# Four layers on four images: the 4x4 convolution for images 3 and 4, exchanged attention operands in fourteen query blocks, and hand-set paces

## The chip, the cores and the metric

The kernel runs on one core of one Trainium2 chip. The metric is device time in microseconds for one execution; the time of the kernel before is the median of three runs. A core has a matrix engine (TensorE, PE in the profile), a vector engine (VectorE, DVE), an activation engine (ScalarE, ACT), a general engine (GpSimd, POOL) and a synchronising engine (SyncE, SP) that here issues DMA transfers. Each engine runs its own instructions in order and waits for others on semaphores. Operands lie in SBUF, products of PE in the eight banks of PSUM, 512 fp32 values per partition each. All data are fp32.

## The reference

Four images of 256 channels and 64x64 pixels pass through four layers, each `x = x + layer(groupnorm32(x))`:

```python
# layer 0: 3x3 convolution, group norm, relu, then attention over all 4096 pixels
xs = relu(group_norm(conv3x3(x, smooth_w) + smooth_b, 8 groups))
g, theta, phi = (conv1x1(xs, w, b) for each)            # 128 channels each
y = softmax(theta^T phi) @ g                             # 4096 x 4096, per image
return 0.1 * group_norm(conv1x1(y, w_w), 32 groups) + xs
# layer 1: linear attention, 4 heads of 32, rms norms before and after
# layer 2: a 3x3 depthwise kernel and a 256x256 pointwise matrix, both generated from the image
# layer 3: softmax-weighted mixture of four 256x256 matrices
```

The softmax needs, for each query pixel, a sum over 4096 keys. Layer 0's attention and convolution are most of the matrix work.

## The kernel before

Channels lie on partitions, in two halves of 128 (`h`). The image being worked on is in `big` and `xp`; intermediate images go through DRAM (`xs_d`, `wy_d`).

**Order of the work.** No scheduler decides the order: the kernel is a Python program that issues instructions in the order in which they go to the engines. Long pieces of work are generators. `attend(b)` is the attention of image `b`: eight query blocks of 512 pixels (`q`), each in 16 steps (`m`) of 256 keys, so 128 steps. A step issues the two logits products of the *next* step (`pf`, L1021), their exponentials on ACT (`pr`, L1022), two products with `g` that accumulate into one PSUM bank (`py`, L1129), and one DVE addition of the probabilities into `tot` (helper line L132). Between two steps of `attend(b)` a `Chain` issues a piece of other work: what is left of image `b-1` (`tail`: `nonlocal_out`, `linear_attention`, generated layer, experts) and then the convolution of image `b+1`. The other work's generators `yield n`, which adds `n * rate` to a credit; each whole credit is one attention step. `yield None` waits for exactly one step, and `later(n, f)` runs `f` after `n` steps. After an image's attention, `project()` makes `theta`, `phi` (`ps_tp`, L957) and `g` (`ps_g`, L962) of the next image. The last image's tail runs with no attention beside it.

**Convolution.** All images use a Winograd form. Image 1 has `convolve_first`. Image 2 (`b == 1`) has `convolve_second`, with tiles of 4x4 outputs in planar layout: 18 products, each a pair of transformed filters times 8 matmuls of 256 columns (`planar_joiner`, L601). Images 3 and 4 have `convolve`, with tiles of 4x2 outputs: 24 products of 4 matmuls of 512 columns (L529). DVE makes the transformed input `v` and joins the products. Transformed filters `u` are read from DRAM a product ahead, on SP's queue in `convolve_second`, on ACT's (L495) in `convolve`. The closing relu (`normed_relu`) is one ACT instruction per 1024 columns (L703), or four strided ones for image 2 (L698).

**End of a query block.** For `q < 7`, `ended_by_dram` writes the sums over 128 partitions to DRAM (`sum_d`), reads them turned, reduces and inverts them, sends them through DRAM again (`rec_d`) so that every partition holds them, multiplies (`yq`) and does the output product `ps_wy` (L1073); some 14 steps lie between its start and end. For `q == 7`, `ended` sums over partitions by a product with ones (`pss`, L1089), and takes a reciprocal of 128x512 on DVE (L1099).

**Statistics** for the group norms are mostly `bn_stats` on DVE. A `guard` array collects the sizes of sums and reciprocals; if they left a range, a general version of the kernel would run after, which in these runs does not happen.

Of the kernel before, what the change touches and what calls it, by code (L numbers as in the profile page):

```python
# [13 lines left out]
P = 128  # L14
# [24 lines left out]
RW = MX * (IX + 1)  # L39

# [6 lines left out]
class Chain:  # L47
# [3 lines left out]
    def __init__(self, layers, rate=1.0, held=()):  # L51
        self.layers, self.rate, self.due = layers(self), rate, []
        self.held, self.unsettled = held, []
# [28 lines left out]
    def steps(self):  # L82
        credit = 0.0
        for part in (self.layers, self.pending()):
            for n in part:
                if n is None:
                    credit += self.rate - 1
                    yield
                    self.tick()
                    continue  # L90
                credit += n * self.rate
                while credit >= 1:
                    credit -= 1
                    yield
                    self.tick()
# [3 lines left out]
def conv_preact_fast(ctx: ExitStack, tc: tile.TileContext, guard, x, wc, wtpg, ww, wqkv, wout, w1cat, wd2,  # L99
# [44 lines left out]
    tpg = cp.tile([P, 3, N], F32, name="tpg")  # L144
    ra = cp.tile([P, NH, IY, RW], F32, name="ra")
    rt = cp.tile([P, NH, IY, RW], F32, name="rt")
    theta, phi, g = tpg[:, 0, :], tpg[:, 1, :], tpg[:, 2, :]
# [106 lines left out]
    tpgf = tpg.rearrange("p k n -> p (k n)")  # L254
# [80 lines left out]
    def stats_tile():  # L335
        return sp.tile([P, NH, 8, 6], F32, name="st")
# [7 lines left out]
    def warm(n):  # L344

        if n:
            ps = bank("ps_warm")
            for i in range(2 * n):
                nc.tensor.matmul(ps[:, 0:P], ones, ident, start=(i == 0), stop=(i == 2 * n - 1))

# [141 lines left out]
    def load_filter(a, k, last):  # L492

        u = filter_tile("u")
        (nc.scalar if last == 3 else nc.sync).dma_start(out=u, in_=rows_d[a, :, :, 0 if k == 0 else 2] if k in (0, last) else filters[a, :, k - 1])  # L495
        return u
# [88 lines left out]
    def planar_joiner(st):  # L585
# [3 lines left out]
        def stats(k):  # L589
            for oh in range(NH):  # L590
                for s in range(2):
                    nc.vector.bn_stats(st[:, oh, 2 * k + s, :], outs[:, oh, k, bass.ts(s, 2), :])

        def products(pair, v, u):
# [9 lines left out]
            if pair != (0, 5):  # L604
                parts[pair] = k4("sums").rearrange("p (k n) -> p k n", k=2)
                nc.scalar.mul(parts[pair][:, 0], banks[0], -1 / 6 if pair == (1, 2) else 1 / 24)
            return banks

        def joined(a, pair, ps, end):
# [11 lines left out]
            elif not end:  # L621
                s = parts[pair]
# [3 lines left out]
            else:  # L626
                near, far = parts[1, 2], parts[3, 4]
# [10 lines left out]
        return products, joined, rows_joined, operations, stats  # L638

    def input_stats():  # L640

        st = stats_tile()
        for h in range(NH):
            for c in range(8):
                nc.vector.bn_stats(st[:, h, c, :], xin[:, h, bass.ts(c, RB), :].rearrange("p y x -> p (y x)"))
                yield 0.3
        return (yield from group_finish(st, avg8, 1e-5))

    def normalise_planar(gm, rstd):
# [5 lines left out]
        for q in range(4):  # L655
            for h in range(NH):
# [3 lines left out]
                if h == 0:  # L660
                    nc.vector.tensor_scalar(to, src, gm[:, 0:1], rstd[:, 0:1], ALU.subtract, ALU.mult)
                else:
                    nc.scalar.activation(to, src, AF.Identity, bias=nb[:, h:h + 1], scale=rstd[:, h:h + 1])
            yield 1
# [18 lines left out]
    def normed_relu(b, st, hops=0):  # L683
# [9 lines left out]
        def piece(c, h):  # L693
            cols = bass.ts(c, CH)
            if b == 1:
# [15 lines left out]
    def convolve(w, b):  # L711

        def load_filters(i):
            a, k = PRODUCTS[i]
            u = load_filter(a, k, 3)
            return lambda oh, h: u[:, h, bass.ts(oh, P)]

        turning[0] = nc.sync
        PRODUCTS = [(a, k) for a in range(TY) for k in ACROSS1]
        us = load_filters(0)  # L720
        _, gm, rstd = yield from input_stats()
        yield from normalise(gm, rstd)
        for c in (0, HW + 1):
            nc.gpsimd.memset(ra[:, :, :, c:c + 1], 0.0)
        st = stats_tile()
        products, joined, _, rows_joined, joining, stats = joiner(st, 0.5)

        rest = []
# [5 lines left out]

        def multiply(a, k, v, u):
            ps = products(a, k, v, u)
            if k != 1:
                w.later(1, lambda: join(a, k, ps))

        def join(a, k, ps):  # L740
            dst = joined(a, k, ps)
            if k == 3 and a == 4:

                for oh in range(NH):
                    rest.extend(joining(a, oh, dst[oh]))
                for j in range(4):
                    w.later(1 + j, lambda: some(3))
                for j in range(3):
                    w.later(5 + j, lambda j=j: stats(j))
            elif k == 3 and a == 2:  # L750
                for oh in range(NH):
                    rest.extend(joining(a, oh, dst[oh]))
                for j in range(3):
                    w.later(1 + j, lambda: some(2))
            elif k == 3:
                some(len(rest))
                for oh in range(NH):
                    w.later(1, lambda oh=oh: rows_joined(a, oh, dst[oh]))

        for i, (a, k) in enumerate(PRODUCTS):  # L760
            if i % 4 == 3 and i < 16:
                copy_x(b, i // 4)
            if k == 1:
                for op, *args in down_plain(a, ra, ra):
                    op(*args)
                    yield 0.35
            v, u = across_plain(k, ra), us
            if i + 1 < len(PRODUCTS):
                us = load_filters(i + 1)
            w.later(1, lambda a=a, k=k, v=v, u=u: multiply(a, k, v, u))  # L770
            yield 0.8
        yield from w.pending()
        turning[0] = nc.scalar
        stats(3)
        yield from normed_relu(b, st, 1)

    def convolve_second(w):

        _, gm, rstd = yield from input_stats()
        yield from normalise_planar(gm, rstd)  # L780
        st = stats_tile()
        products, joined, rows_joined, joining, stats = planar_joiner(st)
        PRODUCTS = [(a, pair) for a in range(TY) for pair in PAIRS]

        rest = []

        def some(n):
            for _ in range(min(n, len(rest))):
                op, *args = rest.pop(0)
                op(*args)  # L790

        def multiply(a, pair, v, u, after):
            ps = products(pair, v, u)
# [3 lines left out]
        def join(a, pair, ps):  # L797
            dst = joined(a, pair, ps, False)
            if pair == (3, 4):
                if a == 5:  # L800
                    some(len(rest))
                w.later(1, lambda: joined(a, pair, ps, True))
            elif pair == (1, 2):
                pass
            elif a == 4:
# [5 lines left out]
                for j in range(3):  # L811
                    w.later(5 + j, lambda j=j: stats(j))
# [5 lines left out]
            else:  # L818
                some(len(rest))
                for oh in range(NH):  # L820
                    w.later(1, lambda oh=oh: rows_joined(a, oh, dst[oh]))

        def load_one(us, i, n):
            if i < len(PRODUCTS):
                a, pair = PRODUCTS[i]
                us.append(load_filter(a, pair[n], 5))

        us = []
        for n in range(2):
            load_one(us, 0, n)  # L830
        for i, (a, pair) in enumerate(PRODUCTS):
            if pair == PAIRS[0]:

                pace = 1.8 if a == 5 else 0.87
                for op, *args in down(a, planar, ra, rt, ra):
                    op(*args)
                    yield 0.75 * pace
            (v, ops), u, us = across(pair), us, []
            load_one(us, i + 1, 0)
            if i % 3 == 2 and i < 12:  # L840
                copy_x(1, i // 3)
            for op, *args in ops:
                op(*args)
                yield 0.4 * pace
            w.later(1, lambda a=a, pair=pair, v=v, u=u, after=lambda us=us, i=i: load_one(us, i + 1, 1): multiply(a, pair, v, u, after))
            yield pace
        yield from w.pending()
        stats(3)
        yield from normed_relu(1, st, 1)

    def convolve_first(w):
# [51 lines left out]
        sums = sp.tile([P, 2, NH, 2], F32, name="sums", bufs=1)  # L903
# [23 lines left out]
        def moments():  # L927

            mv = sp.tile([P, NH, 2], F32, name="mv")
            both = sp.tile([P, 2, NH], F32, name="both_m", bufs=1)  # L930
            sq = sp.tile([P, NH], F32, name="sq_m", bufs=1)
            for h in range(NH):
                nc.vector.bn_aggr(mv[:, h, :], st[:, h, 0:4, :].rearrange("p c s -> p (c s)"))
            nc.vector.tensor_reduce(both, sums, AX.X, ALU.add)
            nc.vector.tensor_scalar(both, both, 1.0 / N, None, ALU.mult)
            mean, var = mv[:, :, 0], mv[:, :, 1]
            tt(mean, mean, minus, ALU.add)
            tt(sq, mean, mean, ALU.mult)
            tt(var, var, sq, ALU.add)
            stt(var, var, 0.5, both[:, 1, :], ALU.mult, ALU.add)  # L940
            stt(mean, mean, 0.5, both[:, 0, :], ALU.mult, ALU.add)
            tt(sq, mean, mean, ALU.mult)
            tt(var, var, sq, ALU.subtract)
            tt(mean, mean, minus, ALU.subtract)
            return mv

        yield from normed_relu(0, moments)


    def project():  # L950

        for c in range(N // 512):
# [11 lines left out]
            tt(g[:, cols].rearrange("p (j o) -> p j o", o=P), ps, bg_s.unsqueeze(1).to_broadcast([P, 4, P]), ALU.add)  # L964
# [5 lines left out]

    turning = [nc.scalar]
# [1524 lines left out]
```

## Time and profile before

| | |
|---|---|
| median of three runs | 3008.09 us (3007.47 to 3008.75) |
| the profiled execution | 3005.05 us, its span 3003.3 us |
| PE busy | 2953.0 us, 98% of the span |
| DVE busy | 2058.4 us, 69% |
| ACT busy | 1192.8 us, 40% |
| logits `pf`, 512 columns | 2048 records |
| `py`, 512 columns | 2048 records |
| `ps_conv`, 4x2 form of images 3 and 4 (`u`), 512 columns | 384 records |
| `ps_conv`, 4x4 form of image 2, 256 columns | 288 records |
| image 1's convolution and projection | to about 181 us |
| attention of image 1 with the convolution of image 2 | 181 to 697 us |
| attention of image 2; image 3's convolution from 1223 | 744 to 1423 us |
| attention of image 3; image 4's convolution from 1946 | 1467 to 2146 us |
| attention of image 4 | 2190 to 2752 us |
| tail of image 4 | 2752 to 3003 us |

A matmul in fp32 is two records in the trace. Records of PE overlap: a record lasts from its issue to its modelled end, so what one matmul costs is read from the distance between the starts of consecutive ones. PEld is the loading of the stationary operand. In lists of groups the columns are busy time and mean duration of one, then the idle time of the engine just ahead of them and what ended it. In the table by stretch each engine has its busy time and, in brackets, its instructions.

### The profile page before, as it was taken

Reading aid. Unit: us, or ns where it says so; the run is one execution under the profiler, and the core shown is the slowest. Engines: PE = TensorE matmul, PEld = TensorE weight load, DVE = VectorE, ACT = ScalarE, POOL = GpSimd, SP = SyncE. Lnnn points to the kernel's source line nnn. Section 1 sums busy time; section 2 is a strip of 40 time slices with the busy share of each in tenths; the row PEclk is TensorE's granted clock in tenths of the full one; section 3 lists DMA queues with packets and bytes.
Section 4 is the critical chain, followed back from the end, with each engine's and each line's share of the span. In section 5 each row is a group of like instructions: output and inputs, shape, how many; then the busy total and the mean of one; then the engine's idle time right before and its main releaser. Section 6 shows DMA issues by size and latency. Waiting matters only on the chain.

```text
span 3003.3 us, 25088 instructions
## 1 busy us (share of the span) xinstructions
PE 2953.0 (98%) x8750; PEld 1511.7 (50%) x8750; DVE 2058.4 (69%) x2835; ACT 1192.8 (40%) x2318; POOL 132.3 (4%) x182
## 2 busy tenths in 40 slices
PE   7999999999999999999999999999999999999998
PEld 3454555555565444444566444444546644444744
DVE  8747667773646994778455797578655468886585
ACT  2234333335456333322455533412335454333732
POOL 0000000001001000000001000000000100000100
PEclk9999999999999999999999999999999999999999
DMA  5245534224402225431610334243431222244021
GB/s 225 76 98 114 60 60 77 39 35 100 90 4 36 32 25 140 86 72 35 161 8 11 53 20 88 78 88 67 89 101 14 25 42 46 28 95 91 22 70 68
DMA packets 536133, 200.58 MB, mean 67 GB/s; under 512 B 471040, under 2 KB 481024, under 8 KB 532480
## 3 DMA queue, kind: packets, MB, share of 16 engines
q1 hardware_dynamic: 127808, 163.25, 17.6%
q10 hardware_dynamic: 403584, 18.88, 12.0%
q0 software_dynamic: 4608, 16.78, 3.7%
q8 instruction: 71, 1.16, 0.2%
q14 instruction: 62, 0.51, 0.1%
HBM read 130.13 MB, written 85.52 MB: 72 GB/s over the span
## 4 chain that ended last, share of the span: by engine, by line
PE 81%; DVE 12%; issue 5%; ACT 1%; POOL 0%; DMA 0%; DVEq 0%; POOLq 0%; ACTq 0%
PE pf L1021 25%; PE py L1129 24%; PE ps_conv L529 5%; PE ps_tp L957 4%; PE ps_qk L1303 3%; PE ps_ex L1804 3%; PE ps_pw L1577 3%; DVE tot L132 2%; DVE dw L135 2%; PE ps_conv L601 2%; PE ps_ctx L1330 2%; PE ps_g L962 2%; PE ps_o L1399 2%; PE ps_wy L1073 2%; PE ps_dw L1624 1%
## 5 line engine op out<-in xcount | busy, mean ns | idle before, releaser
L1022 ACT ACTIVATE pr<-pf 128x512 f32<-128x512 f32 x1024 | 603.1, 596 | 1092.0 <-PE pf L1021 1034.3
L1021 PE MATMUL pf<-tpg 128*128 128x512 f32 x2048 | 966.3, 594 | 0.0
L1129 PE MATMUL py<-pr,tpg 128*128 128x512 f32 x2048 | 961.7, 592 | 0.0
L132 DVE TENSOR_TENSOR tot<-tot,pr 128x1024 f32<-128x1024 f32 x448 | 546.5, 1220 | 181.8 <-ACT pr L1022 181.0
L1129 PEld LDWEIGHTS py<-pr,tpg 128*128 128x128 f32 x2048 | 389.2, 190 | 489.7 <-issue 481.6
L1021 PEld LDWEIGHTS pf<-tpg 128*128 128x128 f32 x2048 | 383.0, 190 | 428.4 <-issue 407.3
L135 DVE SCALAR_TENSOR_TENSOR dw<-xp,dk,dw 128x1008 f32<-128x1008 f32 x208 | 263.1, 1268 | 6.7 <-ACT dw L1569 3.6
L529 PE MATMUL ps_conv<-v,u 128*128 128x512 f32 x384 | 170.9, 593 | 3.2 <-DVE v L132 3.2
L132 DVE TENSOR_TENSOR tpg<-ps_g,bg_s 128x512 f32<-128x512 f32 x32 | 22.1, 692 | 146.9 <-PE ps_g L962 146.9
L529 PEld LDWEIGHTS ps_conv<-v,u 128*128 128x128 f32 x384 | 72.8, 190 | 95.8 <-issue 89.1
L957 PE MATMUL ps_tp<-big,wtpg_s 128*128 128x512 f32 x256 | 116.3, 594 | 2.7 <-ACT big L698 2.0
L225 POOL TENSOR_TENSOR rstd<-rstd,half 128x2 f32<-128x2 f32 x24 | 17.5, 729 | 2194.4 <-DVE rstd L382 2070.5
L1303 PE MATMUL ps_qk<-wqkv_s,xg 128*128 128x256 f32 x496 | 113.1, 379 | 0.0
L1303 PEld LDWEIGHTS ps_qk<-wqkv_s,xg 128*128 128x128 f32 x496 | 94.0, 190 | 21.3 <-issue 8.6
L1577 PE MATMUL ps_pw<-dw,pk 128*128 128x512 f32 x216 | 98.0, 593 | 0.9 <-DVE dw L135 0.9
L958 ACT ACTIVATE tpg<-ps_tp,btp_s 128x512 f32<-128x512 f32 x64 | 44.0, 687 | 95.3 <-PE ps_tp L957 95.3
L957 PEld LDWEIGHTS ps_tp<-big,wtpg_s 128*128 128x128 f32 x256 | 46.6, 190 | 54.5 <-issue 45.2
L1313 ACT ACTIVATE qk<-ps_qk,rinv 128x256 f32<-128x256 f32 x100 | 46.9, 474 | 65.2 <-PE ps_qk L1303 62.9
L962 PEld LDWEIGHTS ps_g<-wtpg_s,big 128*128 128x128 f32 x512 | 62.2, 192 | 15.3 <-issue 15.3
L132 DVE TENSOR_TENSOR v<-ra 128x1024 f32<-128x1024 f32 x58 | 69.2, 1221 | 0.3
L1812 ACT ACTIVATE res<-ps_ex,b 128x512 f32<-128x512 f32 x56 | 38.2, 687 | 76.0 <-PE ps_ex L1804 72.4
L1577 PEld LDWEIGHTS ps_pw<-dw,pk 128*128 128x128 f32 x216 | 40.9, 190 | 53.2 <-issue 49.7
(391 smaller groups left out, 3099.0 us busy)
## 6 DMA issues: line engine op xcount, KB each, us to landing
xp<-in_x_dram SPq DMA_DIRECT2D x16, 1024.0 KB, 8.1
xs_d<-big POOLq DMA_DIRECT2D x32, 512.0 KB, 6.4
wy_d<-wt SPq DMA_DIRECT2D x32, 512.0 KB, 2.8
wy<-wy_d SPq DMA_DIRECT2D x32, 512.0 KB, 4.0
out_dram<-res SPq DMA_DIRECT2D x64, 256.0 KB, 2.0
xs_d<-in_x_dram SPq DMA_DIRECT2D x24, 512.0 KB, 6.0
xs<-xs_d SPq DMA_DIRECT2D x24, 512.0 KB, 4.7
wp<-in_wp_dram SPq DMA_DIRECT2D x16, 512.0 KB, 5.3
```

What stands on the lines that cost most here:

```text
L132: nc.vector.tensor_tensor(o, a, b, op)
L135: nc.vector.scalar_tensor_tensor(o, a, s, b, op0, op1)
L529: nc.tensor.matmul(ps[oh], u(oh, h), v[:, bass.ts(h, 512)], start=(h == 0), stop=(h == NH - 1))
L601: nc.tensor.matmul(ps[:, bass.ts(oh, IY * IX)], u[i][:, h, bass.ts(oh, P)], v[:, i, bass.ts(h, IY * IX)], start=(h == 0), stop=(h == NH - 1))
L957: nc.tensor.matmul(ps, wtpg_s[:, h, k, :], big[:, h, cols], start=(h == 0), stop=(h == NH - 1))
L962: nc.tensor.matmul(ps[:, j, :], big[:, h, bass.ts(4 * c + j, P)], wtpg_s[:, h, 2, :], start=(h == 0), stop=(h == NH - 1))
L1021: nc.tensor.matmul(pf, phi[:, bass.ts(2 * m + s, P)], theta[:, bass.ts(q, 512)], start=True, stop=True)
L1022: nc.scalar.activation(pr[:, bass.ts(s, 512)], pf, AF.Exp)
L1129: nc.tensor.matmul(py, g[:, bass.ts(2 * m + s, P)], probs[i][:, bass.ts(s, 512)], start=(m == 0 and s == 0), stop=(m == NM - 1 and s == 1))
L1303: nc.tensor.matmul(ps[:, 0:2 * HID], xg[:, h, bass.ts(j, P)], wqkv_s[:, h, 0:2 * HID], start=(h == 0), stop=(h == NH - 1))
L1577: nc.tensor.matmul(ps, pk[:, h * NH * P + oh * P:h * NH * P + (oh + 1) * P], dw[h][:, bass.ts(s, 512)], start=(h == 0), stop=(h == NH - 1))
L1804: nc.tensor.matmul(ps, wm[h][:, bass.ts(oh, P)], big[:, h, bass.ts(c, 512)], start=(h == 0), stop=(h == NH - 1))
```

## The change

- **Convolution.** `convolve_second` becomes `convolve(w, b, pace)` and serves images 2, 3 and 4; the 4x2 form is gone. `pace` is 0.87 for image 2 and 0.53 for the others. For `b > 1` it is *metered*: its steps yield 0, and `owe(us)` adds to `w.owed` the time of what was issued, in units of 4.35 us, which `Chain.steps` puts to the credit. A list `begun` holds a product back (`yield None`) while the one before has not been issued. Filters are on SP's queue for all three images. Planar normalising for `b > 1` shares its pieces between DVE and ACT, and the relu for all of images 2 to 4 is in four strided pieces.
- **Attention.** In blocks for which `across(q)` holds (`q == 7` in every image, and `q >= 2` in images 2 and 3: 14 of 32) the operands of `py` are exchanged: a 128x128 slice of the probabilities is the stationary operand and a tile of `g` moves, four matmuls of 129 columns for one of 512. `g` has a column of ones behind each 128, so that column 129 of the product is the row sum. `py` takes two banks, `tot` is not summed, and a new `ended` divides, transposes back (`ps_yt`, four per block) and does `ps_wy`, with no trip through DRAM.
- **Statistics.** In `nonlocal_out`, the generated layer and the convolution, sums come from `accum_out` of the DVE addition and of ACT's squares, joined by two helpers.
- **Paces.** The chains' rates go from 1.33, 0.83 and 1.2 to 1.365, 0.775 and 1.14; several yields change by some hundredths to tenths; `copy_x` of the image after next moves into the loop of the linear attention.

```diff
@@ class Chain, steps
             for n in part:
+                credit += self.owed
+                self.owed = 0.0
                 if n is None:
@@ normalise_planar
-                if h == 0:
-                    nc.vector.tensor_scalar(to, src, gm[:, 0:1], rstd[:, 0:1], ALU.subtract, ALU.mult)
+                if h == 0 or b > 1 and q % 2:
+                    nc.vector.tensor_scalar(to, src, gm[:, h:h + 1], rstd[:, h:h + 1], ALU.subtract, ALU.mult)
@@ normed_relu
-            if b == 1:
+            if b > 0:
@@ convolve
+        metered = b > 1
+
+        def owe(us):
+            if metered:
+                w.owed += us / US_A_STEP
...
             (v, ops), u, us = across(pair), us, []
-            load_one(us, i + 1, 0)
+            load_filter_of(us, i + 1, 0)
...
             for op, *args in ops:
                 op(*args)
-                yield 0.4 * pace
-            w.later(1, lambda ...: multiply(a, pair, v, u, after))
-            yield pace
+                owe(0.12 + 0.0011 * args[0].free_size())
+                yield 0 if metered else 0.4 * slow
+            if begun:
+                yield None
+            begun.append(i)
+            w.later(1, lambda ...: multiply(a, pair, v, u, after))
+            yield 0 if metered else slow
@@ attend
+        def ended(q, py, xc):
+            total, r = (sp.tile([P, 4], F32, name=name) for name in ("total", "r_q"))
+            for i in range(2):
+                nc.vector.tensor_copy(total[:, bass.ts(i, 2)], py[i][:, :, P])
+            nc.vector.reciprocal(r, total)
+            yn = k2("yn")
+            tt(yn[:, 0:2 * P].rearrange("p (t o) -> p t o", o=P), py[0][:, :, 0:P],
+               r[:, 0:2].unsqueeze(2).to_broadcast([P, 2, P]), ALU.mult)
+            for t in range(2, 4):
+                nc.scalar.activation(yn[:, bass.ts(t, P)], py[1][:, t - 2, 0:P], AF.Copy, scale=r[:, t:t + 1])
...
             yield
+            pt, yt = bank("ps_yt"), k2("yt")
+            for t in range(4):
+                nc.tensor.transpose(pt[:, bass.ts(t, P)], yn[:, bass.ts(t, P)], ident)
...
+        def across(q):
+            return q == NQ - 1 or 0 < b < B - 1 and q >= TURNED
...
             for s in range(2):
-                nc.tensor.matmul(py, g[:, bass.ts(2 * m + s, P)], probs[i][:, bass.ts(s, 512)],
-                                 start=(m == 0 and s == 0), stop=(m == NM - 1 and s == 1))
-            if m == 1:
+                begin, end = m == 0 and s == 0, m == NM - 1 and s == 1
+                if across(q):
+                    for t in range(4):
+                        nc.tensor.matmul(py[t // 2][:, t % 2, :], probs[i][:, s * 512 + t * P:s * 512 + (t + 1) * P], g[:, 2 * m + s, :],
+                                  start=(begin and t % 2 == 0), stop=(end and t % 2 == 1))
+                else:
+                    nc.tensor.matmul(py, g[:, 2 * m + s, 0:P], probs[i][:, bass.ts(s, 512)], start=begin, stop=end)
+            if across(q):
+                pass
+            elif m == 1:
@@ nonlocal_out
         for i, (c, h) in enumerate(PARTS):
-            added(i, sc)
+            added(i, sc, accum_out=sums[:, 0, h, c:c + 1])
...
-            yield 0.7
-            for s in range(2):
-                nc.vector.bn_stats(st[:, h, 2 * c + s, :], big[:, h, bass.ts(2 * c + s, 512)])
-            yield 0.7
+            w.later(1, lambda c=c, h=h: squares(c, h))
+            yield 1.3
@@ the order of the whole
-            run(Chain(both(*parts), 1.33 if b == 0 else 0.83).steps(), attention)
+            run(Chain(both(*parts), 1.365 if b == 0 else 0.775).steps(), attention)
...
-        run(Chain(tail(B - 2, big, qT, held=held), 1.2).steps(), attention)
+        run(Chain(tail(B - 2, big, qT, held=held), 1.14).steps(), attention)
```

## The prediction

> **What bounds the kernel now.** First the page's shares and the forty slices.
>
> ```profile
> span 3003.3 us, 25088 instructions
> ...
> PE 2953.0 (98%) x8750; PEld 1511.7 (50%) x8750; DVE 2058.4 (69%) x2835; ACT 1192.8 (40%) x2318; POOL 132.3 (4%) x182
> ...
> PE   7999999999999999999999999999999999999998
> ...
> DVE  8747667773646994778455797578655468886585
> ```
>
> TensorE (PE) is full in every slice but the first and last; VectorE (DVE) has room nearly everywhere. Next the table of busy time by stretch: convolution of image 2, the tail of image 1, convolution of image 3, the last tail.
>
> ```profile
> 181.00:693.00 512.00, 512.00 (x1348) 254.97 (x1347) 356.77 (x445) 184.45 (x302) 5.42 (x7) 1.00 0.37 64
> 745.00:1200.00 455.00, 453.24 (x1361) 234.03 (x1360) 315.44 (x440) 203.31 (x426) 24.55 (x29) 1.00 0.30 54
> 1223.00:1420.00 197.00, 194.78 (x457) 86.09 (x456) 162.65 (x190) 50.47 (x84) 2.32 (x3) 1.00 0.35 67
> ...
> 2752.00:3003.00 251.00, 232.22 (x905) 140.43 (x903) 167.18 (x316) 112.74 (x297) 20.52 (x29) 1.00 0.18 63
> ```
>
> First number length, then PE, weight loads, DVE, ACT. Between 181 and 2752 us PE idles some 2 us per segment and the clock stays at 1.00, so a saving there is PE's passes and little else. Then PE's waits, to see what can still be won there:
>
> ```profile
> PE ps_conv L529 <- DVE v L132: 3.2, 2, 1.6
> ...
> PE ps_wy L1073 <- DVE yq L132: 2.2, 2, 1.1
> PE ps_tp L957 <- ACT big L698: 2.0, 3, 0.7
> ```
>
> Last the timeline, because durations overlap and only the distance between starts counts. A matmul in fp32 appears as two records, here called passes.
>
> ```profile
> 330.12 3.62 PE L601 MATMUL ps_conv<-v,u 128*128 128x256 f32 x16
> 333.57 1.88 PE L1021 MATMUL pf<-tpg 128*128 128x512 f32 x4
> ...
> 153.29 1.95 PE L962 MATMUL ps_g<-wtpg_s,big 128*128 128x128 f32 x16
> ```
>
> From start to start: (333.57−330.12)/16 = 216 ns per pass of 256 columns; (1.88−0.59)/3 = 429 ns for 512; (1.95−0.28)/15 = 112 ns for 128. Each row has a weight load per pass.
>
> [...] the one- and two-column passes (L364) also keep 111 to 112 ns apart. [...]
>
> **The sum, against the profiled 3005.05 us** (span 3003.3; the median 3008.09 lies 3.0 above and I carry that over).
>
> 1. Convolution of images 3 and 4. Per image 24 products of 4 matmuls of 512 columns, 192 passes × 429 = 82.4 us, become 18 products of 8 matmuls of 256, 288 × 216 = 62.2. Twice −20.2: **−40.4**.
>
> 2. Turned blocks. q = 7 in all four images and q = 2 to 6 in images 2 and 3 are 14 of 32 blocks, each of 32 slices: 448 slices. A slice was one matmul, 2 × 429 = 858 ns; it becomes four of 129 columns, 8 passes. This pitch is not in the trace. From below 112 ns [...], from above 219 (the 257-column row L1330, absurd) or, more reasonably, 125 if a row of 129 floats or the two-bank output costs something. 256 and 257 columns differ by 3 ns, 128 is at 112: I take 113. 448 × (904−858) = **+20.4**; each nanosecond more adds 3.6.
>
> 3. Block ends. 56 transposes × 109 ns (L1429's pitch) = +6.1; four pss go, 8 × 429 = −3.4. ps_wy stays 64 matmuls. **+2.7**.
>
> 4. Projections of images 3 and 4. Their relu becomes four strided ACT pieces (607 ns pitch, 2.4 us) for one of 1.23. In image 2's projection, with this form, PE stood 3.0 us longer than its passes' pitches sum to (three waits of ps_tp on big, the 2.0 us above, and what starting again takes); images 3 and 4 lost 0.1 and 0.2. I take +1.5 each, since the rest of the loop is the same but the first pieces are ready earlier: **+3** (0 to +6).
>
> 5. Stalls. The new loop holds a product back until the one before has begun, so L529's first wait (1.6 us in each of images 3 and 4) should go, and the yq waits go where blocks are turned: with pw −0.6 each, −7. Added: nonlocal_out's squares sit on ACT ahead of exponentials and wait for `about` from DVE (some 0.9 us, twice), the planar normalise puts 2.17 us pieces on ACT (0.5), first relus and first v (1.2): +3.5. **−3.5**. All estimates.
>
> 6. The end. Between the last py and the statistics of the last block (2753.9 to the pm at 2761.6) stands now pss 0.87, reciprocal 3.37, two scalings 1.29, two statistics 1.19: 6.7 us. After: total and r 0.85, yn 0.5, transposes and four ps_ex in between 3.4, ps_wy 1.7, copy 0.6, statistics 0.6: 8.6. **+2**.
>
> Sum −15.8; the conv's filters arriving on SP instead of ACT's queue also take 48 issues from ACT (0.3 to 0.6 us each in the timeline, 22 us over two images), a small gain for exponentials that I count at −1. **−17**: profile 2988, median **2991**.
>
> Costed at nothing: DVE loses the sums `tot` of 14 blocks (15 × 1.22 us each, 256 us) and most bn_stats, less what the 4x4 transforms add: by the durations before, some 110 of the 507 us that it is busy in the 723 us from one projection's end to the next (743.9 to 1466.9). PE did not wait for these, so none of it is time. ACT takes squares instead (0.6 to 0.85 us each, near 45 us more in the same stretch, on 286): hidden under PE while an exponential is ready before its py. A step is 4.3 us or more, its exponentials 1.2, logits run one step ahead, so about 2 us of lateness is covered; two squares in a row are 1.7. Were cover gone, 16 parts × 1 us × 2 images would cost 32. SP's queue gets 36 filter loads per image of images 3 and 4 that it did not have, behind its xs and wy transfers (2.8 to 6.0 us landing by the page), each issued a product ahead (some 10 us); if one came late, its product would wait that long. The row sums' DRAM round trip goes from 28 blocks to 18; its yields stay. Paces and owed steps only place work: a bad place shows as v or ps_conv late by one DVE operation, 1.2 us, per product; 36 products, so at worst 43 us.
>
> **Rivals.**
> - *Bigger gain, near 2980:* the projection loses nothing (−3), the new stalls do not come (−3.5), and the mid-segment gaps of 5.3 us go altogether. For: DVE 110 us lighter. Against: the trace blames PE waits on DVE for only some microseconds in all. 0.13.
> - *No gain, near 3006:* the paces or ACT's queue give it back. Late exponentials for two squares per part cost 0.5 us each over 32 parts, or 0.4 us per product over 36: about +15. For: FIFO on ACT, `about` made on DVE, image 3's v lateness of 1.6 us today. Against: 181 to 693 us ran the same 18 planar products with DVE 70% busy without one gap. 0.13.
> - *Slower, 3019:* one mechanism, the 129-column pass. Beyond 112 ns each nanosecond is 3.6 us; the gain is gone at 113 + 17/3.6 = 117.7 ns, and at 121 ns (8% over the floor, from the odd row length or alternating between two banks) it is +29 − 17 = +12 us, 3019. For: nothing in the trace has such a pass. Against: 128 columns at 112, 256 to 257 at 216 to 219. 0.14.
> - *The turn does not lighten anything:* the exchanged products cost PE 20 us for DVE time that is idle; then the change would be best without it. This is part of my forecast, not another time.
>
> **How the numbers follow.** The likeliest, −17 within 8 (items 2, 4 and 5 carry ±4, ±3, ±5): 0.60, own range 2983 to 2999. Bigger 0.13, none 0.13, slower 0.14. The range 2980 to 3010 leaves out about 0.07 below and 0.12 above. This kernel's measurement tells 0.2%, 6 us. Faster: all of bigger, the likeliest, and a little of none: 0.74; same 0.12; slower 0.14.
>
> **What would show it.** 1: the row of ps_conv with 128x256 has 864 passes, and no row of ps_conv<-v,u with 512 is left; 216 ns apart. 2: py with 128x129 has 3584 passes, read from start to start at 112 to 114; at 118 or more the sum falls. 4: PE's waits of ps_tp on big 3 to 9 us in all. 5: v waits absent at the start of both later convolutions; a wait of py on pr names the rival of the squares. 6: a distance near 8.6 us after the last py. Though DVE's share falls to about 60%, PE should stay at 98%. Wrong if PE's idle time in 745 to 2752 us grows by over 10 us, or the pitch passes 117 ns.

## The result and the profile after

The changed kernel takes 2986.53 us (median of four runs, 2985.65 to 2988.41) against 3008.06 us; the ratio is 0.9929, with an interval of 0.9912 to 0.9946. That is 21.5 us less, where 17 were forecast. Its profiled execution took 2988.41 us, with a span of 2986.7.

From the page of the changed kernel, the span, PE's share and the forty slices of PE and DVE:

```profile
span 2986.7 us, 31274 instructions
...
PE 2934.1 (98%) x11678; PEld 1785.7 (60%) x11678; DVE 1798.8 (60%) x2785; ACT 1328.7 (44%) x2674; POOL 136.8 (5%) x185
...
PE   7999999999999999999999999999999999999998
...
DVE  8737667751645854675455583667154568854584
```

PE is as full as before; DVE lost 260 us of work. Set beside DVE's row of before, shown with the prediction, the three 9s (slices 14, 15 and 24, the depthwise taps of images 1 and 2) are gone. Those slices turn out to matter.

PE's waits between 181 and 2727 us, with the total, the count and the longest:

```profile
PE ps_tp L951 <- ACT big L760: 4.0, 6, 0.7
...
PE py L1126 <- ACT pr L1014: 2.4, 2, 1.2
PE ps_conv L663 <- DVE v L137: 2.3, 2, 1.2
```

The waits of L529 and of ps_wy on `yq` are gone. In their place the first product of each later convolution waits 1.2 us for `v`, one `py` near the end of the segment waits 1.2 us for exponentials that stand behind relu pieces on ACT, and three projections instead of one wait for the strided relu.

The pitch of the new products, from the timeline (start, duration, count):

```profile
1404.82 1.95 PE L1126 MATMUL py<-tpg,pr 128*128 128x129 f32 x16
...
1413.27 1.95 PE L956 MATMUL ps_g<-wtpg_s,big 128*128 128x128 f32 x16
```

Sixteen passes of 129 columns take exactly as long as sixteen of 128, 1.95 us. Over all 3584 passes of 129 columns the median distance between starts is 112.0 ns.

By stage, from the first record of each attention or projection to the next, the last tail from the last logits product on (profiled executions):

| stage, us | before | changed | ten blocks back (e1) | best (e10) |
|---|---|---|---|---|
| attention 1, convolution 2 | 515.4 | 517.1 | 517.1 | 517.1 |
| projection 2 | 47.2 | 45.8 | 45.8 | 43.9 |
| attention 2, tail 1, convolution 3 | 678.7 | 665.5 | 677.1 | 664.7 |
| projection 3 | 44.3 | 45.8 | 45.8 | 43.9 |
| attention 3, tail 2, convolution 4 | 678.8 | 665.6 | 675.9 | 664.7 |
| projection 4 | 44.3 | 45.8 | 45.8 | 43.9 |
| attention 4, tail 3 | 560.1 | 560.2 | 560.2 | 560.2 |
| tail 4 | 253.2 | 259.5 | 257.8 | 254.4 |

The gain is in the two segments that hold the changed convolutions, 13.2 us each. The last tail takes 253.2 us in before's profiled execution, which ran at a mean granted clock of 1.000 and 3 us under its median, and 259.5 us in the changed kernel's, which ran at 0.997 and 1.9 us over its own; with the same code there it is 254.5 us in e11's execution, at 0.999. So the spans of the two profiles differ by 16.6 us where the medians differ by 21.5.

### The profile page after: what moved, and what is told of

Same layout as the page of the kernel before. It is cut to its first block, busy times and chain, and to the rows that moved or that the text cites. A ratio compares the mean times of both kernels' runs of the same rounds, so it can differ in the third digit from the quotient of the medians.

```text
span 2986.7 us, 31274 instructions
## 1 busy us (share of the span) xinstructions
PE 2934.1 (98%) x11678; PEld 1785.7 (60%) x11678; DVE 1798.8 (60%) x2785; ACT 1328.7 (44%) x2674; POOL 136.8 (5%) x185
## 4 chain that ended last, share of the span: by engine, by line
PE 76%; issue 19%; DVE 2%; ACT 2%; POOL 0%; DMA 0%; ACTq 0%; DVEq 0%; POOLq 0%
PE pf L1013 24%; PE py L1129 16%; PE py L1126 8%; PE ps_tp L951 4%; PE ps_ex L1811 4%; PE ps_qk L1316 3%; PE ps_pw L1580 3%; PE ps_conv L663 2%; PE ps_ctx L1343 2%; PE ps_o L1414 2%; PE ps_g L956 2%; PE ps_dw L1631 1%; PE ps_wy L1066 1%; ACT big L760 1%; PE ps_xt L1296 1%
## 5 line engine op out<-in xcount | busy, mean ns | idle before, releaser
L1013 PEld LDWEIGHTS pf<-tpg 128*128 128x128 f32 x2048 | 374.1, 190 | 358.4 <-issue 336.4
L1129 PE MATMUL py<-pr,tpg 128*128 128x512 f32 x1152 | 541.6, 592 | 0.9 <-ACT pr L1014 0.9
L1126 PEld LDWEIGHTS py<-tpg,pr 128*128 128x128 f32 x3584 | 434.9, 192 | 108.0 <-issue 100.7
L1126 PE MATMUL py<-tpg,pr 128*128 128x129 f32 x3584 | 436.3, 275 | 2.4 <-ACT pr L1014 2.4
L1129 PEld LDWEIGHTS py<-pr,tpg 128*128 128x128 f32 x1152 | 218.6, 190 | 277.4 <-issue 268.3
L137 DVE TENSOR_TENSOR tot<-tot,pr 128x1024 f32<-128x1024 f32 x252 | 307.6, 1221 | 98.5 <-ACT pr L1014 98.0
L663 PE MATMUL ps_conv<-v,u 128*128 128x256 f32 x864 | 195.6, 379 | 2.3 <-DVE v L137 2.3
L663 PEld LDWEIGHTS ps_conv<-v,u 128*128 128x128 f32 x864 | 161.5, 190 | 31.3 <-issue 8.4
L140 DVE SCALAR_TENSOR_TENSOR sums<-ps_conv,sums 128x512 f32<-128x512 f32 x72 | 49.8, 691 | 103.9 <-PE ps_conv L663 97.5
L1316 PEld LDWEIGHTS ps_qk<-wqkv_s,xg 128*128 128x128 f32 x496 | 93.8, 190 | 20.4 <-issue 8.4
L1580 PE MATMUL ps_pw<-dw,pk 128*128 128x512 f32 x216 | 97.4, 592 | 0.0
L951 PEld LDWEIGHTS ps_tp<-big,wtpg_s 128*128 128x128 f32 x256 | 45.8, 190 | 54.7 <-issue 41.8
```

The source lines that it names most:

```text
L137: nc.vector.tensor_tensor(o, a, b, op)
L140: nc.vector.scalar_tensor_tensor(o, a, s, b, op0, op1)
L663: nc.tensor.matmul(ps[:, bass.ts(oh, IY * IX)], u[i][:, h, bass.ts(oh, P)], v[:, i, bass.ts(h, IY * IX)], start=(h == 0), stop=(h == NH - 1))
L951: nc.tensor.matmul(ps, wtpg_s[:, h, k, :], big[:, h, cols], start=(h == 0), stop=(h == NH - 1))
L1013: nc.tensor.matmul(pf, phi[:, bass.ts(2 * m + s, P)], theta[:, bass.ts(q, 512)], start=True, stop=True)
L1126: nc.tensor.matmul(py[t // 2][:, t % 2, :], probs[i][:, s * 512 + t * P:s * 512 + (t + 1) * P], g[:, 2 * m + s, :], start=(begin and t % 2 ...
```

## The experiments

All are changes of the changed kernel. Times are medians, to be set against 2986.53 us.

### e1: ten blocks back to 512 columns

```diff
-TURNED = 2
+TURNED = 7
```

> Only the last block of each image keeps its operands exchanged; ten blocks of images 2 and 3 go back to 512 columns, tot and the trip through DRAM. Theory (PE's passes alone set the time, freed DVE time is worth nothing): each block gives back 32 x 38 ns and four transposes of 109 ns, 1.66 us, so -16.6 us on the changed kernel: 2970, and no wait on DVE over 3 us in all. Rival (the exchange is what keeps DVE ahead of the 4x4 convolution): the sums put back 92 us of DVE work per middle segment, DVE goes to about the same load as PE where the convolution runs, and its waits eat the 16.6 us: 2985 or more, with PE waits on v, ps_conv or dw.

Measured 3009.84 us (3006.86 to 3010.53): 23 us slower, though PE has 16.6 us less to do. The rival holds. PE's waits in this run:

```profile
PE ps_pw L1580 <- DVE dw L140: 17.4, 6, 7.1
...
PE ps_conv L663 <- DVE v L137: 8.1, 2, 4.1
...
PE ps_conv L663 <- DMA u<-rows_d: 3.6, 2, 1.9
```

The busy times by stretch, for the depthwise taps (about step 48 to 64 of an attention) and for the convolution (from step 80), first of the changed kernel, then of this run; the columns are length, PE, weight loads, DVE, ACT, POOL, clock, DMA share and GB/s:

```profile
993.60:1072.40 78.80, 78.80 (x379) 51.06 (x378) 66.07 (x78) 32.96 (x61) 0.00 (x0) 1.00 0.02 7
1167.50:1378.10 210.60, 209.44 (x1118) 160.72 (x1117) 152.16 (x211) 72.90 (x129) 2.95 (x4) 1.00 0.16 51
```

```profile
992.30:1081.70 89.40, 80.69 (x181) 34.98 (x180) 88.34 (x98) 32.09 (x59) 0.00 (x0) 0.94 0.18 15
1175.40:1388.40 213.00, 206.30 (x705) 125.59 (x704) 189.05 (x239) 70.34 (x121) 2.94 (x4) 0.99 0.35 59
```

With the sums `tot` back, DVE is busy 88.3 of 89.4 us in the stretch of the taps: there it is DVE, not PE, that sets the pace, and this stretch alone is 10.6 us longer. In the convolution DVE is busy 189 of 213 us and PE still 206; what is lost there lies in single waits, for `v` at its start and for one filter. The waits themselves add to some 15 us per segment; more is lost after them, with the clock at 0.50 (see the last section).

### e2: all blocks of images 2 and 3 exchanged

```diff
-TURNED = 2
+TURNED = 0
```

> All eight blocks of images 2 and 3 exchanged, four more than in the changed kernel. Theory: 4 x 1.66 us more of PE, +6.6: 2993. Rival (DVE relief pays): less than +3, or a gain.

Measured 2993.08 us (2992.28 to 2994.17), +6.6 as the price of a block on PE says, 4 × 1.66. By stage the two segments are 3.9 and 3.5 us longer. In blocks 0 and 1 the relief of DVE is worth nothing.

### e3: the 4x2 convolution back

```diff
-            parts = [tail(b - 1, big, qT), lambda w: convolve(w, b + 1, 0.53)] if b > 0 else [
+            parts = [tail(b - 1, big, qT), lambda w: convolve_old(w, b + 1)] if b > 0 else [
```

(`convolve_old` is the `convolve` of before with its filter loads, its yields scaled by 0.83/0.775 for the new rate.)

> The changed kernel with the 4x2 convolution of before for images 3 and 4 (filters on ACT's queue, relu in one piece), everything else kept. Theory: the convolution is worth 40.4 us, its strided relu costs 3.0 in the projections, so +37 us: 3024, within 5. Rival (part of the 40 was lost to DVE or ACT in the new form): +25 or less, 3012 or less.

Measured 3016.07 us (3015.37 to 3018.86): +29.5, between the two. By stage the segments are 682.9 and 683.0 us, 17.4 longer each, and the projections 43.9, 1.9 shorter each; 2 × (17.4 − 1.9) = 31. PE's own 20.2 us per image are in the segments, less 1.3 us for the wait for `v` and 1.3 for the late exponentials, neither of which the old form has in this surrounding: 17.6.

### e4: ps_ex behind ps_wy at the end

```diff
         for part, _ in enumerate(attention):
-            if part == 0:
+            if part == 1:
                 end.fill(2)
```

> The changed kernel; in the last block's end the four ps_ex matmuls are issued behind ps_wy instead of between the transposes and ps_wy. Theory: ps_wy then starts when yt is copied, 2.3 us earlier, and the chain of statistics behind it with it: 2984, between 2982.5 and 2985. Rival (the place only moves the idle time of PE, since ps_ex has to be done before the next products anyway): within 0.7 us of the changed kernel.

Measured 2985.84 us (2984.86 to 2987.78), 0.7 less: the rival's bound, and no more than the spread of the runs. ps_wy does start 2.4 us earlier (1.6 us after the transposes began, for 3.9), PE waiting 0.9 us for `yt` ahead of it. But the product `pm` for the statistics comes 7.7 us after the transposes began, for 8.0: the four ps_ex now stand ahead of it. The rival's reason is what the trace shows.

### e5: ten blocks back, without their sums

```diff
-            elif m > 1:
+            elif m > 1 and not (0 < b < B - 1 and q >= 2):
                 tt(tot, tot, probs[i], ALU.add)
```

(with TURNED = 7)

> As the run with ten blocks exchanged back, and in these ten blocks the sums tot beyond the first pair of steps are left out (the row sums there are then too small), so DVE has the load of the changed kernel and PE that of the run before. Theory A (tot on DVE is what stalled it): PE's sum, 2986.5 - 16.6 = 2970, up to 2974. Theory B (the trip through DRAM, PSUM banks or the paces stall it): within 8 us of 3009.8.

Measured 2978.09 us (2975.48 to 2980.41), 32 us under e1; this is 4 us outside theory A's range, and theory B is refuted. The same two stretches, of the taps and of the convolution, in this run:

```profile
992.40:1069.70 77.30, 77.30 (x182) 34.25 (x181) 68.70 (x79) 32.70 (x59) 0.00 (x0) 1.00 0.21 17
1163.20:1373.00 209.80, 205.12 (x707) 124.62 (x706) 157.26 (x211) 70.55 (x121) 2.95 (x4) 1.00 0.35 59
```

In the taps PE no longer has a gap. The segments are 661.1 us, 16.0 and 14.8 under e1's, and most of the difference to the changed kernel's segment less the price of five blocks (665.5 − 8.3 = 657.2, called PE's sum here) is in waits that stay: 1.9 us per segment for `v` and 1.8 for a filter from DRAM. That last wait is in the three runs with ten blocks back and not in the changed kernel; a filter's load then shares SP's queue with the trips of the row sums, which is the likely cause but was not tried. The additions to `tot` explain some 15 of e1's 20 us per segment over PE's sum (677.1 − 657.2).

### e6: ten blocks back, with paces made for them

```diff
-EASED = 0.68
+EASED = 1.0
-US_A_STEP = 4.35
+US_A_STEP = 5.0
```

(with TURNED = 7)

> Ten blocks exchanged back again, with paces for it: taps not eased (EASED 1.0 for 0.68), an attention step counted as 5.0 us for 4.35 in the metered convolution. Theory A (DVE's sum in a stage is the bound: in the convolution about 148 us of its own and 36 of tot, against 165 of PE in 30 steps): waits on dw go, waits on v come, 3000 to 3012. Rival (only the paces were wrong, the sum has room: 490 of 660 us in a segment): 2970 to 2980.

The taps then take more attention steps, and the convolution, whose work is counted at 5.0 us a step, is issued in fewer. Measured 3008.75 us (3007.66 to 3009.67), 1.1 under e1 and in theory A's range. The waits move and do not go:

```profile
PE ps_tp L951 <- ACT big L760: 14.9, 12, 4.5
...
PE ps_conv L663 <- DVE v L137: 6.1, 2, 3.1
PE ps_conv L663 <- DMA u<-filters: 3.2, 3, 1.5
...
PE ps_pw L1580 <- DVE dw L140: 2.3, 2, 1.2
```

The taps are served (2.3 us for 17.4). The waits for `v` did not grow, as theory A had it, but fell from 8.1 to 6.1; instead the convolution ends so late that the projection waits up to 4.5 us for its relu. One retiming is not a search, so another might do better; with this one, what the taps gained was lost at the end of the convolution.

### e7: half of the strided relu on DVE

```diff
+                    if k % 2 and c > 0:
+                        nc.vector.tensor_scalar(to, src, sc[:, h:h + 1], sh[:, h:h + 1], ALU.mult, ALU.add)
+                        nc.vector.tensor_scalar(to, to, 0.0, None, ALU.max)
+                    else:
+                        nc.scalar.activation(to, src, AF.Relu, bias=sh[:, h:h + 1], scale=sc[:, h:h + 1])
```

> The changed kernel; in the projections of images 2 to 4 half of the strided relu pieces (those behind the first 1024 columns) are two DVE instructions instead of one on ACT. Theory: the six waits of ps_tp on big, 4.0 us and 5.6 us of wall over the pitches, go: 2981.5, between 2980.5 and 2983. Rival (ACT's own two copies per block of ps_tp are the limit): no more than 1 us.

Measured 2994.14 us (2993.65 to 2995.46): 7.6 *slower*, a miss of both. The timeline of the third projection, first of the changed kernel, then of this run:

```profile
1431.87 2.63 ACT L760 ACTIVATE big<-xp,sh,sc 128x256 f32<-128x256 f32 x4
...
1434.55 2.84 PE L951 MATMUL ps_tp<-big,wtpg_s 128*128 128x512 f32 x6 [0.67 <-ACT big L760]
```

```profile
1435.81 0.69 DVE L137 TENSOR_TENSOR tpg<-ps_g,bg_s 128x512 f32<-128x512 f32 x1 [1.62 <-PE ps_g L959]
1436.42 0.51 DVE L763 TENSOR_SCALAR big<-xp,sc,sh 128x256 f32<-128x256 f32 x1
...
1438.34 1.95 PE L954 MATMUL ps_tp<-big,wtpg_s 128*128 128x512 f32 x4 [1.71 <-DVE big L764]
```

On DVE the piece stands behind the addition to `g`, which waits for ps_g. It starts at 1436.4, not at the relative place at which ACT could begin, and PE waits 1.7 us for it instead of 0.7. An idle engine is no help if the queue in front of the work waits for PE itself. The same pieces ahead of that addition were not tried.

### e8: block 4 back

```diff
-            return q == NQ - 1 or 0 < b < B - 1 and q >= TURNED
+            return q == NQ - 1 or 0 < b < B - 1 and q >= TURNED and q != 4
```

> The changed kernel with q = 4 of images 2 and 3 exchanged back, the block in whose steps DVE is 32 to 42% busy. Theory A (an exchange is only worth something where DVE is near full): two blocks give back 1.66 us each, 2983.2. Rival (any block put back costs its share of what ten cost, 23 us / 10 each): 2991.

Measured 2983.7 us (2982.37 to 2986.38). The rival is refuted. That theory A is met to 0.5 us is in part chance: by stage the segments are only 0.8 and 0.9 us shorter, 1.7 in all of the 3.3 forecast, since `py` now waits 4.3 us for exponentials in place of 2.4 (for `v` 1.1 in place of 2.3); the rest of the 2.8 is not in the segments. The worth of an exchange depends on its place: in block 4, in which DVE is busy 30.5 of 95.3 us in the changed kernel, it costs more than it brings; the ten blocks of e1 brought 4 us each on average, for a cost of 1.66.

### e9: the relu piece ahead of a block's products

```diff
         for c in range(N // 512):
             cols = bass.ts(c, 512)
+            if relus:
+                relus.pop(0)()
             for k in (1, 0):
...
-            if relus:
-                relus.pop(0)()
             yield
```

> The changed kernel; in the projections the next relu piece is issued ahead of a block's ps_tp products and their copies, not behind them. Theory: a piece waits for the block's own copies by its place in ACT's queue, not for ACT's load; issued first it is done a block early, the six waits of ps_tp on big go, 5.6 us of wall: 2981, between 2980 and 2983. Rival (ACT has too much to do in a block, 2.65 and 1.4 us of 5.2): no more than 1.5 us.

Measured 2980.61 us (2979.92 to 2983.62), as expected. The six waits of ps_tp on `big` are gone and each projection takes 43.9 us for 45.8. The load of ACT is the same; only the place in its queue changed.

### e10: the three together

> The relu pieces first, q = 4 exchanged back, and ps_ex behind ps_wy at the end. If the three are independent: -5.6, -2.8 and -0.7 on 2986.5, so 2977.4, within 2.

Measured 2977.65 us (2976.68 to 2979.26), the sum of the three. Against the kernel before the ratio is 0.9904 (0.9889 to 0.9919), so this version is better than both.

### e11: fixed yields in the later convolutions

```diff
-        metered = b > 1
+        metered = False
```

(with pace 0.66 for 0.53)

> The changed kernel; the convolutions of images 3 and 4 take fixed yields like image 2's (pace 0.66, about the same number of attention steps) instead of owed times. Theory (the same work in the same steps, only its place inside them differs, DVE at 0.8 of PE there): 0 to 4 us slower, 2986.5 to 2990.5. Rival (the owed times are what keeps v ahead): one DVE operation late per product, 36 x 0.5 us or more, 3004 or more.

Measured 2983.38 us (2981.69 to 2984.04): 3.2 *faster*, outside both. The segments are 664.1 us, 1.4 shorter each. The first product of the third image's convolution in the changed kernel and in this run:

```profile
1192.44 3.72 PE L663 MATMUL ps_conv<-v,u 128*128 128x256 f32 x16 [1.16 <-DVE v L137]
```

```profile
1193.24 1.95 PE L1126 MATMUL py<-tpg,pr 128*128 128x129 f32 x16
1195.02 3.62 PE L663 MATMUL ps_conv<-v,u 128*128 128x256 f32 x16
```

With fixed yields the first product comes 2.2 us later in its segment (450.3 us after its start for 448.1), and the wait is gone. The owed steps are thus not what holds the convolution together; at its start they are slightly too tight.

### e12: bn_stats back in nonlocal_out

```diff
-            added(i, sc, accum_out=sums[:, 0, h, c:c + 1])
+            added(i, sc)
...
-            w.later(1, lambda c=c, h=h: squares(c, h))
-            yield 1.3
+            yield 0.7
+            for s in range(2):
+                nc.vector.bn_stats(st[:, h, 2 * c + s, :], big[:, h, bass.ts(2 * c + s, 512)])
+            yield 0.6
```

> The changed kernel with nonlocal_out's statistics back as bn_stats on DVE, 16 of 0.6 us per image, and no squares on ACT there. Theory (that stage has DVE 62 to 71% busy, so it is worth nothing): 2986 to 2987. Rival (any DVE work put back costs time): 2991 or more.

Measured 2989.75 us (2989.44 to 2991.67): +3.2, between the two. The segments are 670.1 and 668.4 us, 4.6 and 2.8 longer. In this profile the last tail is 5.0 us shorter than in the changed kernel's, with the same instructions (mean granted clock of the execution 0.998, for 0.997), so the +3.2 is not the price of the stage alone. The average load of DVE in that stage was the wrong thing to read. PE waits 2.1 us for the moments at the stage's end (`pm` on `mv`) in each of the two segments, and the table by stretch shows the wait and what follows it, first of image 2's attention, then of image 3's:

```profile
785.00:788.00 3.00, 1.03 (x3) 0.19 (x1) 2.97 (x7) 0.00 (x0) 0.00 (x0) 1.00 0.01 5
788.00:792.00 4.00, 3.87 (x8) 1.79 (x9) 2.90 (x7) 1.20 (x2) 0.00 (x0) 0.66 0.00 0
```

```profile
1501.00:1504.00 3.00, 0.93 (x3) 0.10 (x1) 2.97 (x7) 0.00 (x0) 0.00 (x0) 1.00 0.00 0
1504.00:1508.00 4.00, 3.98 (x13) 2.07 (x14) 2.78 (x6) 1.20 (x2) 0.00 (x0) 1.00 0.00 0
```

DVE is full (2.97 of 3 us) just there both times. In the 4 us behind it the clock is at 0.66 the first time and at 1.00 the second, and the first segment is the longer of the two by 1.7 us.

## Why the prediction was right, and where it was wrong

The time is in the likeliest case's own range, 4.5 us under its centre. By its steps:

**1, the convolution.** Right on PE: 864 passes at 216 ns. The worth of the whole part, undone by e3, is 29.5 us and not 37; 2.6 us per image go to the two waits that came in (`v`, late exponentials).

**2, the turned blocks.** The rival of the expensive 129-column pass is refuted. The pitch is 112.0 ns, so the step costs 448 × (896 − 858) = 17.0 us, where 20.4 was taken (448 × 46 ns is 20.6). e2 gives the same price per block. Of what the rival feared, neither the row of 129 floats nor the output in two banks shows: ps_g's passes of 128 columns have the same 112 ns. That 112 ns is a floor under every pass was not shown: in 14 of the 24 products of L364 in before's trace the two passes start 28 to 29 ns apart, and only from the second to the next instruction is it 111 to 112 ns.

**3, the block ends.** The transposes are 109 ns apart, as taken.

**4, the projections.** +1.5 us for images 3 and 4, to the tenth. Not foreseen: image 2's became 1.4 us shorter, one of its three waits being gone. e9 shows that all of it was a matter of order.

**5, the stalls.** In a middle segment the gaps on PE of before that I could see (1.8, 1.3, 0.8, 0.6, 0.4 us) sum to 4.8, the changed kernel's (1.3, 1.3, 0.5) to 3.1. Twice −1.7 is the −3.5 of the sum, though its parts differ: the wait for `v` at the start of the two convolutions, whose absence was to be a sign, is there with 1.2 us each, and a `py` stood behind relu pieces more than one behind squares.

**6, the end.** The last tail is 1.3 us longer than before's in an execution with a mean clock of 0.999 (254.5 us in e11, with the same code there), for +2 taken. In the profile of the changed kernel it is 6.3. The parts listed for the end add to 7.65 us and not to the 8.6 written there. From the last `py` to `pm` it is some 9 us (2731.2 to 2740.3), where it was 7.7 before.

**The total.** That the sum of −17 stands beside −16.6 between the two profiles is chance: the changed kernel's last tail was 5.0 us longer in its profile than in e11, which has the same code there. Without that the two profiles would be 21.6 us apart, as the medians are (21.5). So carrying the 3.0 us between profile and median over was sound, and the sum itself was 4.5 us too small. The pitch of the new pass (3.4) and image 2's projection (1.4) are as much as that; smaller errors cancel.

**Costed at nothing: wrong.** "PE did not wait for these, so none of it is time", and, among the rivals, "the change would be best without it": e1 shows the opposite. Ten exchanged blocks cost PE 16.6 us, and without them the kernel is 23 us slower, a difference of 40 us that I had valued at nothing. e5 puts most of that on the sums `tot`. The same two stretches of before, taps and convolution, as the table by stretch gives them:

```profile
992.10:1064.50 72.40, 70.87 (x165) 30.99 (x164) 71.45 (x76) 24.70 (x39) 0.00 (x0) 1.00 0.25 26
1221.80:1390.30 168.50, 166.88 (x390) 73.69 (x389) 138.41 (x149) 38.95 (x67) 0.00 (x0) 1.00 0.38 73
```

PE hardly waited *before*, but in the taps DVE was at the brink, 71.5 of 72.4 us with 76 instructions. The changed kernel issues most of the taps in 0.68 of their steps; with the sums back (e1) DVE has 98 instructions in these 16 steps and needs 88.3 us for them. In the convolution DVE was busy for 0.82 of the stretch before; e1 has 0.89, the changed kernel 0.72. That the tighter taps need the relief that the exchange gives is shown by e1, e5 and e6; for the convolution the same is argued from these shares and from the wait for `v`, 4.1 us in e1 and 1.9 in e5. The page had it: the 9s in DVE's slices, which I read past with "DVE has room nearly everywhere". The forecast came out right because both parts were in the change together; forecasts of one without the other by the same sum failed (e1: 2970 expected, 3009.84 measured; e3: 3024 within 5 expected, 3016.07 measured).

**Paces.** "Only place work" held in the sense that they decide a few us: e11 gains 3.2 us by dropping the owed steps. In e6, the one retiming that was tried, a pace did not buy back work that a stage lacks room for.

## What to carry to other kernels

An engine with 60 to 70% of the span can be the bound in a stage (DVE, 69% of the span before, was busy 71.5 of 72.4 us in the taps): before valuing work taken from it at nothing, read the table by stretch for the stages that the change will make shorter, not only the waits of the kernel as it is. A part of a change that looks like a loss on the bounding engine may be what lets another part be a gain; undo the parts one at a time. And before moving work to an idle engine, look at what the instruction ahead of it in that engine's queue waits for: moving the same relu one place earlier on the busy engine won 5.9 us, moving it to the idle one lost 7.6.

## What was not expected of the hardware

A wait of PE can cost more than its length. In e1, the stretch around the 7.1 us wait for `dw`:

```profile
1057.00:1064.00 7.00, 0.20 (x1) 0.00 (x0) 6.89 (x7) 0.00 (x0) 0.00 (x0) 0.69 0.00 0
1064.00:1066.00 2.00, 1.68 (x2) 0.84 (x3) 2.00 (x3) 0.00 (x0) 0.00 (x0) 0.50 0.00 0
1066.00:1068.00 2.00, 2.00 (x4) 0.78 (x3) 1.96 (x3) 0.00 (x0) 0.00 (x0) 0.50 0.00 0
1068.00:1070.00 2.00, 2.00 (x4) 0.89 (x3) 1.97 (x2) 0.00 (x0) 0.00 (x0) 0.54 0.00 0
1070.00:1072.00 2.00, 2.00 (x6) 0.88 (x5) 2.00 (x3) 0.95 (x2) 0.00 (x0) 1.00 0.00 0
```

The clock, third figure from the end, is at 0.50 to 0.54 for some 5 us after PE has resumed at 1064.32. In it the six passes of 512 columns of L1580 take 5.28 us from the first start to that of the next instruction (1069.60), 0.88 us each; ahead of the wait four such passes take 1.72 us (1054.46 to 1056.18), 0.43 each, so the six cost 2.7 us more. Slow stretches also came after shorter waits: after one of 2.1 us in e12 the clock was at 0.66 in the next 4 us, and at the end of the changed kernel a wait of 1.3 us for the statistics, with some shorter ones around it, was followed by

```profile
2741.00:2745.00 4.00, 3.62 (x8) 1.49 (x8) 3.47 (x21) 0.00 (x0) 1.04 (x1) 0.64 0.35 133
```

while e11, with the same instructions at this place, kept the full clock:

```profile
2738.50:2742.50 4.00, 3.07 (x14) 1.64 (x12) 3.62 (x23) 0.69 (x1) 1.05 (x1) 1.00 0.34 131
```

So the same code may or may not be slowed; the two waits of 2.1 us in e12, one with the clock at 0.66 behind it and one with 1.00, show it inside one execution. What decides between the two is not shown by any run here. In the table by stage the last tail ranges from 253.2 to 259.5 us. That slow stretches are the reason for most of this is an estimate: by the table of busy times by stretch, length times missing clock is 7.4 us in the changed kernel's tail (0.64 over 4 us, 0.91 over three stretches of 66 us together) and 1.3 us in e11's (0.94 over its last 21.7), where the tails take 259.5 and 254.5 us.
